# A gated line scan: its normaliser by Ln, Exp and one Newton step, its directions summed by identity matmuls

## The chip, the cores and the metric

One core of a Trainium2 chip runs the whole program in one launch. The metric is the device time in microseconds (us). Three runs of the kernel before took 17805.31, 17695.79 and 17706.48 us; their median is 17706.48 us.

## The reference

Two layers work on 8 images of 192 x 64 x 64, in float32. The change is in the first, a gated scan in four directions over 384 channels:

```
Gl, Gm, Gr = normalize_w(...)       # s = |Gl| + |Gm| + |Gr| + 1e-7; each of them / s
def step(h, inp):
    x, l, gl, gm, gr = inp          # one column of every chunk of 8
    h_up, h_dn = h shifted by one row down and up, zeros at the border
    hn = l * x + gl * h_up + gm * h + gr * h_dn
    return (hn, hn)
out = hs * Us + xs * Ds             # hs: all hidden states; xs: the input in 4 directions
y = einsum('bdchw,d->bchw', out by direction, w_m)
```

The gates, L, U and D are projections of a 16-channel proxy of the input. Behind the scan come two norms and a projection; the second layer is a window attention that keeps the 16 largest scores of a row, and an MLP.

## The kernel before

For each of the 8 images the program runs four stages. `front` projects the input and convolves it. `scan` works channel tile by channel tile (ct, 3 of 128 channels), step by step (t, 8), direction by direction (d, 4), each time on 512 tokens (64 rows x 8 chunks). `norms` takes the layer norm and the response norm. `window_row` (8 a image) does the second layer.

The scan of one direction at a step t > 0, with the lines of the kernel:

- TensorE projects three gates into one PSUM tile g of three banks (through the helper at L229), and L, D and U into tiles pl of one bank each. A projection has 16 rows: row groups at partitions 0, 32, 64 and 96 hold copies of the proxy.
- VectorE (DVE) multiplies L by the input (lx, L272). ScalarE (ACT) takes the absolute values of the gates (ab, L274). DVE multiplies the gates by the three shifted hidden states (pr, L276).
- GpSimd (POOL) adds two absolute values (L277), DVE adds the third and 1e-7 (L278) and takes the reciprocal (L281).
- POOL adds the three products (L282, L283) and multiplies by the reciprocal (L284). DVE adds lx, which is the new hidden state (`now`, L285).
- DVE multiplies D by the input (dx, L290) and U by the hidden state (hu, L294). POOL adds hu and dx to an accumulator in SBUF (L297, L299, L301); for the last direction the sum goes to y (L303).

At t = 0 there are no gates: L times the input is the hidden state (L269). The hidden states of the four directions are four tiles; the directions do not depend on each other, the steps do.

The program is written with symbolic tiles. A scheduler puts the instructions of each engine into one fixed order, and each engine works its queue in that order. A pool with one buffer makes the next tile wait until the last reader of the one before is done. PSUM has 8 banks, and the scan uses all: g has two buffers (6 banks), pl two.

Of the kernel before, what the change touches and what calls it, by code (L numbers as in the profile page):

```python
# [31 lines left out]
STRIP = 16  # image rows of one convolution strip  # L32
# [9 lines left out]
def tile_ss2d_then_window_attention(ctx: ExitStack, tc: tile.TileContext, a: dict, out: bass.AP):  # L42
    """Layer 0 (gated line scan in four directions) and layer 1 (top-16 window attention and MLP).

    Token orders of one image of 64 x 64, h = row, w = 8 c + t:
      scan order    (t, h, c): a step of the scan is 512 tokens in a row
      window order  (g, c, i, t), h = 8 g + i: a window is 64 tokens, a group 512, in a row
    Heads are taken as h = 2 r + j: r is the partition block of 32, j the block of 96 channels.
    """
# [17 lines left out]
    w_in = load("w_in")  # [96, 2, 384]  # L67
    w_dw = load("w_dw")  # [128, 3, 9]
    vecs = load("vecs")  # [128, 5, 3]: b_dw, gamma, beta, ln_w, ln_b
    w_xd = load("w_xd")  # [128, 3, 128]: x_proxy in four copies, 32 partitions apart  # L70
    w_g1 = load("w_g1")  # rows 0, 32, 64, 96: left, middle, right gate, L
    w_g2 = load("w_g2")  # rows 0, 32: D, U
    w_m = load("w_m", a["w_m"].partition_broadcast(48))
    w_out = load("w_out")  # [128, 3, 192]
    w_qk = load("w_qk")  # [96, 2, 384], columns (qk, j, r, d)
    b_qk = load("b_qk")  # [1, 384]
    w_v = load("w_v")  # [96, 2, 192], columns (j, r, d)
    b_v = load("b_v")  # [96, 2], rows (r, d), columns j
    w_pr = load("w_pr")  # [96, 2, 192], rows (r, d) of j
    b_pr = load("b_pr")  # [1, 192]  # L80
    n1_g = load("n1_g", a["n1_g"].partition_broadcast(P))
    n1_br = load("n1_br")  # [1, 192]
    n_cols = load("n_cols")  # [96, 3, 2]: norm1_b, norm2_g, norm2_b
    temp = load("temp", a["temp"].partition_broadcast(P))  # [128, 6], (j, r)
    rpb = load("rpb")  # [128, 3, 128], (window, query) x r x (j, key)
    w_f1 = load("w_f1")  # [96, 2, 768]
    b_f1 = load("b_f1")  # [128, 6]
    w_f2 = load("w_f2")  # [128, 6, 192]
    b_f2 = load("b_f2")  # [96, 2]
# [10 lines left out]
    nc.vector.memset(eps5, 1e-5)  # L100
    rpb_neg = const.tile([P, 3, P], F32, tag="rpb_neg", name="rpb_neg")
    nc.vector.tensor_scalar(rpb_neg, rpb, NEG, None, ALU.add)
    # One hidden state a direction, with a row of zeros above the image and one below it.
# [5 lines left out]
    with tc.tile_pool(name="prep", bufs=2) as prep, tc.tile_pool(name="prep_ps", bufs=2, space=PSUM) as prep_ps:  # L109
        # The direction's weight goes into its U and D.  # L110
# [3 lines left out]
        # W_out with its outputs' mean taken off, as the norm behind it does.  # L114
# [5 lines left out]
        # norm1's b is left out of the tokens: it goes into the biases of q, k, v and the shortcut.  # L120
# [4 lines left out]
        # v's bias comes out of the attention as it went in: it goes into the projection's.  # L125
# [16 lines left out]
        # norm2's g and b go into fc1.  # L142
# [78 lines left out]
    def scan(xa, xp, y):  # L221
        with (
            tc.tile_pool(name="scan", bufs=2) as pool,
            tc.tile_pool(name="gate_ps", bufs=2, space=PSUM) as gps,
            tc.tile_pool(name="lud_ps", bufs=2, space=PSUM) as lps,
# [11 lines left out]
            def directed(ct, d, t):  # L237
                """The scan's input of direction d at step t, [p, h, c] or [p, h / 8, h % 8, c]."""
                u = CH - 1 - t if d >= 2 else t
                if d % 2 == 0:  # L240
                    v = xa[:, ct, u * 512 : (u + 1) * 512].rearrange("p (i c) -> p i c", c=CH)
                else:
                    v = xa[:, ct, :].rearrange("p (il h ih) -> p ih il h", il=8, ih=8)[:, :, :, u::CH]
                if d >= 2:
                    v = v[:, :, ::-1] if d % 2 == 0 else v[:, :, :, ::-1]
                return v
# [6 lines left out]
            for ct in range(CT):  # L253
                y_ct = y[:, ct, :].rearrange("p (g c i t) -> p g i c t", g=NG, c=CH, i=WS)
                for t in range(CH):
                    acc = pool.tile([P, 512], F32, name="acc")
                    for d in range(ND):
# [3 lines left out]

                        if t > 0:
                            g = gps.tile([P, 3, 512], F32, name="g")
                            for r in range(3):
                                project(g[:, r, :], w_g1, r, ch, t)
                        pl = lps.tile([P, 512], F32, name="pl")
                        project(pl, w_g1, 3, ch, t)
                        if t == 0:
                            nc.vector.tensor_mul(as_directed(now, d), as_directed(pl, d), xv)  # L269
                        else:  # L270
                            lx = pool.tile([P, 512], F32, name="lx")
                            nc.vector.tensor_mul(as_directed(lx, d), as_directed(pl, d), xv)  # L272
                            ab = pool.tile([P, 3, 512], F32, name="ab")
                            nc.scalar.activation(ab, g, AF.Abs)  # L274
                            pr = pool.tile([P, 3, 512], F32, name="pr")
                            nc.vector.tensor_mul(pr, g, view(hid[d], [[CH, 3], [1, 512]]))  # L276
                            nc.gpsimd.tensor_add(ab[:, 0, :], ab[:, 0, :], ab[:, 1, :])  # L277
                            nc.vector.scalar_tensor_tensor(  # L278
                                ab[:, 0, :], ab[:, 2, :], 1e-7, ab[:, 0, :], ALU.add, ALU.add
                            )  # L280
                            nc.vector.reciprocal(ab[:, 0, :], ab[:, 0, :])  # L281
                            nc.gpsimd.tensor_add(pr[:, 0, :], pr[:, 0, :], pr[:, 1, :])  # L282
                            nc.gpsimd.tensor_add(pr[:, 0, :], pr[:, 0, :], pr[:, 2, :])  # L283
                            nc.gpsimd.tensor_mul(pr[:, 0, :], pr[:, 0, :], ab[:, 0, :])  # L284
                            nc.vector.tensor_add(now, pr[:, 0, :], lx)  # L285

                        pd = lps.tile([P, 512], F32, name="pl")
                        project(pd, w_g2, 0, ch, t)
                        dx = pool.tile([P, 512], F32, name="dx")
                        nc.vector.tensor_mul(as_directed(dx, d), as_directed(pd, d), xv)  # L290
                        pu = lps.tile([P, 512], F32, name="pl")
# [4 lines left out]
                        if d == 0:  # L296
                            nc.gpsimd.tensor_add(acc, hu, dx)  # L297
                            continue
                        nc.gpsimd.tensor_add(acc, acc, hu)  # L299
                        if d < ND - 1:  # L300
                            nc.gpsimd.tensor_add(acc, acc, dx)  # L301
                        else:
                            nc.gpsimd.tensor_add(  # L303
                                y_ct[:, :, :, :, t],
                                acc.rearrange("p (g i c) -> p g i c", g=NG, c=CH),
                                dx.rearrange("p (g i c) -> p g i c", g=NG, c=CH),
                            )

# [1 line left out]
    def norms(y, small, one):  # L310
        gx = small.tile([P, CT, NG], F32, name="gx")
        with tc.tile_pool(name="norms", bufs=2) as pool:
            for g in range(NG):
# [20 lines left out]
                # Tokens' scales from partitions to a row, the same on all partitions.  # L334
# [46 lines left out]
    def window_row(b, g, y, wz, bz, pool, small, one, three):  # L381
        def two_blocks(dst, src):
            """The transpose of [128 tokens, tile, 192] as [96 channels, 2, 512 tokens]."""
# [8 lines left out]
        # W_out and norm1  # L392
# [20 lines left out]
        # q and k, each head's to length one  # L413
# [21 lines left out]
        qkT = pool.tile([HALF, 4, GT], F32, name="qkT", bufs=1)  # blocks q0, q1, k0, k1  # L435
# [11 lines left out]
        # v, keys of a window on partitions, once for j = 0 and below for j = 1  # L447
# [16 lines left out]
        # scores: partitions (window of a pair, query), columns (r, pair, j, key); r has a bank  # L464
# [17 lines left out]
        # the 16th largest of each row  # L482
# [12 lines left out]
        # softmax of kept scores or -100, and the position bias  # L495
# [16 lines left out]
        # attention times v, as [(r, d), j, token]  # L512
# [25 lines left out]
        # projection, shortcut, norm2  # L538
# [28 lines left out]
        # MLP, by channels; x2 is added by transposing it onto fc2's sums  # L567
# [53 lines left out]
def _laid_out(i):  # L621
    """The inputs in the layouts that the program reads them in."""
# [16 lines left out]
    # Heads h = 2 r + j: channels (r, j, d) to (j, r, d).  # L639
# [55 lines left out]
```

## Time and profile before

| What | Value |
|---|---|
| median of three runs | 17706.48 us |
| span of the profiled execution, first to last instruction | 17788.9 us |
| the run of the three that is nearest above that span | 17805.31 us |
| busy over the whole span: PE, DVE, POOL, ACT | 12616.1, 8605.7, 5983.4, 3160.3 us |
| period of one image | about 2223 us |
| y of step 0 to y of the last step, in the scan of the first image (POOL L303) | 304.10 to 1137.79 us |
| the same, second image | 2542.66 to 3376.59 us |
| from y to y of a step: channel tile 0; tiles 1 and 2 | 39.95 us; 37.2 us |
| granted TensorE clock, mean over the span | 0.637 |

The profile is of one execution. PE is TensorE's matmuls, PEld its weight loads. A group line gives the busy time and mean duration of its instructions, then the engine's idle time just before them and who ended it. A float32 matmul shows as two MATMUL records, two passes. The clock is the share of full TensorE speed that the throttle granted; the profile shows 0.5 and 1.0, and means between. A timeline line gives start, duration (both us), engine, line, operation, tiles, shapes and count.

### The profile page before, as it was taken

The numbers are of one execution on the slowest core, as the hardware profiler recorded it, in microseconds if no ns is written. First come the engines' busy times: TensorE is split into PE (matmuls) and PEld (weight loads), VectorE is DVE, ScalarE is ACT, GpSimd is POOL, SyncE is SP. The second block draws the span as 40 slices with busy tenths as digits, with TensorE's granted clock in tenths as the row PEclk, the third lists the DMA queues.
The fourth block names the chain that finished last, engine by engine and source line by source line (L and its number), as shares of the span: only waits on it lengthen the run. The fifth ranks groups of instructions, "written<-read, shape, count | busy, mean of one in ns | idle before, by whom it ended". The sixth has DMA issues, their size and how long they took to land. (4 is left out here: it accounts for less than half of the span.)

```text
span 17788.9 us, 115154 instructions
## 1 busy us (share of the span) xinstructions
PE 12616.1 (71%) x44232; PEld 5933.9 (33%) x44232; DVE 8605.7 (48%) x14317; ACT 3160.3 (18%) x4337; POOL 5983.4 (34%) x4570
## 2 busy tenths in 40 slices
PE   8776687766876668776687766876668776687665
PEld 3233332333323333233332333323333233332333
DVE  3952239622395223962239522395223952249522
ACT  1112211122111221112211122111221112211122
POOL 2740027400274002740027400274002740027400
PEclk8556685566755668556685566755668556675566
DMA  0000000000000000000000000000000000000000
GB/s 18 0 0 4 3 9 0 0 4 3 9 0 0 4 3 9 0 0 4 3 9 0 0 4 3 9 0 0 4 3 9 0 0 4 4 8 0 0 4 4
DMA packets 23070, 64.52 MB, mean 4 GB/s; under 512 B 2707, under 2 KB 3286, under 8 KB 22518
## 3 DMA queue, kind: packets, MB, share of 16 engines
q1 hardware_dynamic: 21424, 54.68, 1.2%
q8 instruction: 347, 5.69, 0.1%
q10 hardware_dynamic: 1094, 2.48, 0.0%
q14 instruction: 205, 1.68, 0.0%
HBM read 31.98 MB, written 25.17 MB: 3 GB/s over the span
## 5 line engine op out<-in xcount | busy, mean ns | idle before, releaser
L229 PE MATMUL pl<-xp,w_g 16*128 16x512 f32 x4608 | 3811.1, 1124 | 1306.0 <-DVE dx L290 553.6
L229 PE MATMUL g<-xp,w_g 16*128 16x512 f32 x4032 | 2729.0, 1108 | 456.7 <-DVE pr L276 456.7
L281 DVE RECIPROCAL ab<-ab 128x512 f32<-128x512 f32 x672 | 2244.8, 3340 | 0.0
L501 POOL TENSOR_TENSOR at<-at,rpb 128x1536 f32<-128x1536 f32 x64 | 218.6, 3415 | 5967.1 <-DVE keep L491 5904.6
L229 PEld LDWEIGHTS pl<-xp,w_g 16*128 16x128 f32 x4608 | 1133.8, 307 | 3187.2 <-DVE dx L290 1322.6
L274 ACT ACTIVATE ab<-g 128x1536 f32<-128x1536 f32 x672 | 974.7, 1450 | 5678.3 <-POOL pr L284 5082.3
L518 PE MATMUL one<-ident,ex 128*128 128x128 f32 x768 | 197.2, 427 | 1980.9 <-POOL ex L510 1980.9
L229 PEld LDWEIGHTS g<-xp,w_g 16*128 16x128 f32 x4032 | 975.6, 315 | 1691.3 <-DVE pr L276 1146.5
L194 PE MATMUL pc<-xin,diag 128*128 128x512 f32 x3456 | 1499.3, 592 | 0.0
L276 DVE TENSOR_TENSOR pr<-g,hid 128x1536 f32<-128x1536 f32 x672 | 1175.0, 1749 | 6.5 <-ACT ab L274 6.2
L277 POOL TENSOR_TENSOR ab<-ab 128x512 f32<-128x512 f32 x672 | 850.0, 1265 | 941.3 <-ACT ab L274 941.3
L405 DVE RECIPROCAL ss<-ss 128x4 f32<-128x4 f32 x64 | 11.4, 178 | 2211.7 <-ACT ss L404 2211.7
L283 POOL TENSOR_TENSOR pr<-pr 128x512 f32<-128x512 f32 x672 | 990.4, 1474 | 52.7
L284 POOL TENSOR_TENSOR pr<-pr,ab 128x512 f32<-128x512 f32 x672 | 855.2, 1273 | 311.1 <-DVE ab L281 297.7
L189 DVE COPY xin<-pin 128x384 f32<-128x384 f32 x288 | 160.6, 558 | 1606.3 <-PE pin L182 1606.3
L194 PEld LDWEIGHTS pc<-xin,diag 128*128 128x128 f32 x3456 | 653.0, 189 | 810.1 <-issue 784.8
L282 POOL TENSOR_TENSOR pr<-pr 128x512 f32<-128x512 f32 x672 | 862.1, 1283 | 36.9 <-DVE pr L276 36.9
L578 PE MATMUL one<-hd,w_f 128*96 128x512 f32 x1536 | 809.4, 652 | 56.7 <-ACT hd L576 56.7
L572 PE MATMUL one<-xT,w_f 96*128 96x512 f32 x1536 | 848.0, 680 | 0.0
L518 PEld LDWEIGHTS one<-ident,ex 128*128 128x128 f32 x768 | 146.0, 219 | 2000.6 <-POOL ex L510 1989.6
L299 POOL TENSOR_TENSOR acc<-acc,hu 128x512 f32<-128x512 f32 x576 | 740.6, 1286 | 156.0 <-DVE hu L294 155.9
L285 DVE TENSOR_TENSOR hid<-pr,lx 128x512 f32<-128x512 f32 x672 | 510.3, 759 | 554.6 <-POOL pr L284 554.3
(154 smaller groups left out, 16751.0 us busy)
## 6 DMA issues: line engine op xcount, KB each, us to landing
out_dram<-ot SPq DMA_DIRECT2D x64, 384.0 KB, 3.0
xt<-in_x_dram SPq DMA_DIRECT2D x16, 864.0 KB, 7.4
xt<-in_x_dram SPq DMA_DIRECT2D x16, 816.0 KB, 5.8
w_f<-in_w_f_dram ACTq DMA_DIRECT2D x2, 576.0 KB, 7.5
w_g<-in_w_g_dram SPq DMA_DIRECT2D x1, 768.0 KB
w_g<-in_w_g_dram ACTq DMA_DIRECT2D x1, 768.0 KB
w_in<-in_w_in_dram SPq DMA_DIRECT2D x1, 288.0 KB, 3.3
w_out<-in_w_out_dram ACTq DMA_DIRECT2D x1, 288.0 KB, 10.3
```

Of the source, the lines that this page charges most:

```text
L194: nc.tensor.matmul(pc, lhsT=diag[:, ct, k, :], rhs=xin[:, 8 * hf + dy : 8 * hf + dy + 8, dx : dx + W], start=k == 0, stop=k == 8,)
L229: nc.tensor.matmul(dst, lhsT=w[32 * row : 32 * row + NS, ch : ch + P], rhs=xp[32 * row : 32 * row + NS, t, :], start=True, stop=True,)
L274: nc.scalar.activation(ab, g, AF.Abs)
L276: nc.vector.tensor_mul(pr, g, view(hid[d], [[CH, 3], [1, 512]]))
L277: nc.gpsimd.tensor_add(ab[:, 0, :], ab[:, 0, :], ab[:, 1, :])
L281: nc.vector.reciprocal(ab[:, 0, :], ab[:, 0, :])
L282: nc.gpsimd.tensor_add(pr[:, 0, :], pr[:, 0, :], pr[:, 1, :])
L283: nc.gpsimd.tensor_add(pr[:, 0, :], pr[:, 0, :], pr[:, 2, :])
L284: nc.gpsimd.tensor_mul(pr[:, 0, :], pr[:, 0, :], ab[:, 0, :])
L299: nc.gpsimd.tensor_add(acc, acc, hu)
L572: nc.tensor.matmul(ph, lhsT=w_f1[:, ci, m * P : (m + 1) * P], rhs=xT[:, ci, :], start=ci == 0, stop=ci == 1)
L578: nc.tensor.matmul(pf[k], lhsT=w_f2[:, m, k * HALF : (k + 1) * HALF], rhs=hd, start=m == 0, stop=False)
```

## The change

It touches `scan` (and adds a constant of 1e-7 per partition, eps7). The reciprocal r of s + 1e-7 becomes exp(-ln(s + 1e-7)) on ACT, followed by one Newton step. The sum s is put into the PSUM bank of the right gate; DVE works there. With rr the first estimate and p the sum of products, `gr` becomes (s + 1e-7) rr, then (gr - 2) (p rr), and the hidden state is lx - gr. The three gates lie in two tiles, g (two banks) and gr (one bank), so Abs and the product with the hidden state are two instructions each. L and D share a tile of two banks, U has a tile of its own, and the directions are summed in PSUM by matmuls with the identity: dx and hu of four directions make 8 matmuls onto one bank, and ACT copies it to y. Buffers: g 1 (2 banks), gr 2, L and D 1 (2 banks), U 1, acc 1; all 8 banks again.

```diff
-            tc.tile_pool(name="gate_ps", bufs=2, space=PSUM) as gps,
-            tc.tile_pool(name="lud_ps", bufs=2, space=PSUM) as lps,
+            tc.tile_pool(name="gate_ps", bufs=1, space=PSUM) as gps,
+            tc.tile_pool(name="right_ps", bufs=2, space=PSUM) as rps,
+            tc.tile_pool(name="ld_ps", bufs=1, space=PSUM) as lps,
+            tc.tile_pool(name="u_ps", bufs=1, space=PSUM) as ups,
+            tc.tile_pool(name="acc_ps", bufs=1, space=PSUM) as aps,
...
-                    acc = pool.tile([P, 512], F32, name="acc")
+                    acc = aps.tile([P, 512], F32, name="acc")
...
+                        ld = lps.tile([P, 2, 512], F32, name="ld")
+                        project(ld[:, 0, :], w_g1, 3, ch, t)
+                        project(ld[:, 1, :], w_g2, 0, ch, t)
+                        lx = now if t == 0 else pool.tile([P, 512], F32, name="lx")
+                        nc.vector.tensor_mul(as_directed(lx, d), as_directed(ld[:, 0, :], d), xv)
+                        dx = pool.tile([P, 512], F32, name="dx")
+                        nc.vector.tensor_mul(as_directed(dx, d), as_directed(ld[:, 1, :], d), xv)
...
-                            g = gps.tile([P, 3, 512], F32, name="g")
-                            for r in range(3):
-                                project(g[:, r, :], w_g1, r, ch, t)
...
+                            g = gps.tile([P, 2, 512], F32, name="g")
+                            gr = rps.tile([P, 512], F32, name="gr")
+                            project(g[:, 0, :], w_g1, 0, ch, t)
+                            project(g[:, 1, :], w_g1, 1, ch, t)
+                            project(gr, w_g1, 2, ch, t)
                             ab = pool.tile([P, 3, 512], F32, name="ab")
-                            nc.scalar.activation(ab, g, AF.Abs)
                             pr = pool.tile([P, 3, 512], F32, name="pr")
-                            nc.vector.tensor_mul(pr, g, view(hid[d], [[CH, 3], [1, 512]]))
+                            nc.scalar.activation(ab[:, 0:2, :], g, AF.Abs)
+                            nc.scalar.activation(ab[:, 2, :], gr, AF.Abs)
+                            nc.vector.tensor_mul(pr[:, 0:2, :], g, view(hid[d], [[CH, 2], [1, 512]]))
+                            nc.vector.tensor_mul(pr[:, 2, :], gr, view(hid[d], [[1, 512]], 2 * CH))
                             nc.gpsimd.tensor_add(ab[:, 0, :], ab[:, 0, :], ab[:, 1, :])
-                            nc.vector.scalar_tensor_tensor(
-                                ab[:, 0, :], ab[:, 2, :], 1e-7, ab[:, 0, :], ALU.add, ALU.add
-                            )
-                            nc.vector.reciprocal(ab[:, 0, :], ab[:, 0, :])
                             nc.gpsimd.tensor_add(pr[:, 0, :], pr[:, 0, :], pr[:, 1, :])
                             nc.gpsimd.tensor_add(pr[:, 0, :], pr[:, 0, :], pr[:, 2, :])
-                            nc.gpsimd.tensor_mul(pr[:, 0, :], pr[:, 0, :], ab[:, 0, :])
-                            nc.vector.tensor_add(now, pr[:, 0, :], lx)
...
+                            nc.vector.tensor_add(gr, ab[:, 0, :], ab[:, 2, :])
+                            rr = pool.tile([P, 512], F32, name="rr")
+                            nc.scalar.activation(rr, gr, AF.Ln, bias=eps7)
+                            nc.scalar.activation(rr, rr, AF.Exp, scale=-1.0)
+                            nc.vector.scalar_tensor_tensor(gr, gr, 1e-7, rr, ALU.add, ALU.mult)
+                            nc.gpsimd.tensor_mul(pr[:, 0, :], pr[:, 0, :], rr)
+                            nc.vector.scalar_tensor_tensor(
+                                gr, gr, 2.0, pr[:, 0, :], ALU.subtract, ALU.mult
+                            )
+                            nc.vector.tensor_sub(now, lx, gr)
...
+                        pu = ups.tile([P, 512], F32, name="pu")
                         project(pu, w_g2, 1, ch, t)
                         hu = pool.tile([P, 512], F32, name="hu")
                         nc.vector.tensor_mul(hu, pu, now)
...
-                        if d == 0:
-                            nc.gpsimd.tensor_add(acc, hu, dx)
-                            continue
-                        nc.gpsimd.tensor_add(acc, acc, hu)
...
+                        nc.tensor.matmul(acc, lhsT=ident, rhs=dx, start=d == 0, stop=False)
+                        nc.tensor.matmul(acc, lhsT=ident, rhs=hu, start=False, stop=d == ND - 1)
+                    nc.scalar.copy(y_ct[:, :, :, :, t], acc.rearrange("p (g i c) -> p g i c", g=NG, c=CH))
```

More of the change, by code (lines that the diff above doesn't have):

```diff
@@ L100, in tile_ss2d_then_window_attention @@
     nc.vector.memset(eps5, 1e-5)
+    eps7 = const.tile([P, 1], F32, tag="eps7", name="eps7")
+    nc.vector.memset(eps7, 1e-7)
     rpb_neg = const.tile([P, 3, P], F32, tag="rpb_neg", name="rpb_neg")
@@ L260, in scan @@
                         now = hid[d][:, CH : CH + 512]
-                        if t > 0:
-                            g = gps.tile([P, 3, 512], F32, name="g")
-                            for r in range(3):
-                                project(g[:, r, :], w_g1, r, ch, t)
[L266 to L272, printed above, removed]
+                        ld = lps.tile([P, 2, 512], F32, name="ld")
@@ L283, in scan @@
                             nc.gpsimd.tensor_add(pr[:, 0, :], pr[:, 0, :], pr[:, 2, :])
[L284 to L290, printed above, removed]
@@ L291, in scan @@
-                        pu = lps.tile([P, 512], F32, name="pl")
+                            nc.vector.tensor_add(gr, ab[:, 0, :], ab[:, 2, :])
[4 more added lines that the diff above has]
+                            nc.gpsimd.tensor_mul(pr[:, 0, :], pr[:, 0, :], rr)
@@ L294, in scan @@
                         nc.vector.tensor_mul(hu, pu, now)
-                        if d == 0:
-                            nc.gpsimd.tensor_add(acc, hu, dx)
-                            continue
-                        nc.gpsimd.tensor_add(acc, acc, hu)
[L300 to L307, printed above, removed]
+                        nc.tensor.matmul(acc, lhsT=ident, rhs=dx, start=d == 0, stop=False)
+                        nc.tensor.matmul(acc, lhsT=ident, rhs=hu, start=False, stop=d == ND - 1)
+                    nc.scalar.copy(y_ct[:, :, :, :, t], acc.rearrange("p (g i c) -> p g i c", g=NG, c=CH))
     def norms(y, small, one):
```

## The prediction

> **What bounds the kernel now.** I read the page's busy shares by slice first, then its groups, then the scan alone (the windows view), then single instructions (the timeline).
>
> ```profile
> DVE  3952239622395223962239522395223952249522
> PEclk8556685566755668556685566755668556675566
> ...
> L229 PE MATMUL pl<-xp,w_g 16*128 16x512 f32 x4608 | 3811.1, 1124 | 1306.0 <-DVE dx L290 553.6
> L229 PE MATMUL g<-xp,w_g 16*128 16x512 f32 x4032 | 2729.0, 1108 | 456.7 <-DVE pr L276 456.7
> L281 DVE RECIPROCAL ab<-ab 128x512 f32<-128x512 f32 x672 | 2244.8, 3340 | 0.0
> ```
>
> Eight images repeat. DVE is full (9) only in the scan, and there TensorE's granted clock is 5 tenths. A float32 matmul is two passes: the scan has 2304 `pl` and 2016 `g` matmuls, the page counts 4608 and 4032.
>
> ```profile
> 610.00:1150.00 540.00, 393.68 (x700) 148.42 (x697) 472.75 (x396) 77.00 (x54) 413.73 (x321) 0.50 0.00 0
> ```
>
> This is the scan's second and third channel tile: PE, PEld, DVE, ACT, POOL busy, then the clock. DVE is the bound (88%), PE is busy 73%, ACT 14%. One direction of one step t > 0 (a "turn" below; 84 an image, 672 in all) looks like this:
>
> ```profile
> 744.43 2.07 PE L229 MATMUL pl<-xp,w_g 16*128 16x512 f32 x2 [0.97 <-DVE dx L290]
> ...
> 746.11 0.69 DVE L285 TENSOR_TENSOR hid<-pr,lx 128x512 f32<-128x512 f32 x1 [1.74 <-POOL pr L284]
> 746.72 0.68 DVE L278 SCALAR_TENSOR_TENSOR ab<-ab 128x512 f32<-128x512 f32 x1
> 747.32 0.68 DVE L294 TENSOR_TENSOR hu<-pl,hid 128x512 f32<-128x512 f32 x1
> ...
> 747.92 0.68 DVE L272 TENSOR_TENSOR lx<-pl,xa 128x512 f32<-128x512 f32 x1
> ...
> 748.06 2.67 PE L229 MATMUL pl<-xp,w_g 16*128 16x512 f32 x4 [1.56 <-DVE hu L294]
> 748.52 3.34 DVE L281 RECIPROCAL ab<-ab 128x512 f32<-128x512 f32 x1
> ```
>
> A 512-wide DVE instruction takes 0.68 and the next starts 0.60 after it; one projection (x2) takes 2.07, two on different row groups (x4) 2.67, so the second costs 0.60. POOL's writes of y (L303) at 304.10 and 1137.79 enclose 833.7 us in every image: 84 turns and two t = 0 steps of some 13 each (a step and the t = 0 step behind it take 48.9 and 52.3 there against 37.2 for a step alone). A turn costs (833.7 - 27) / 84 = 9.6.
>
> **What goes, what comes.** Per turn DVE loses the reciprocal (3.26 from start to start) and L278, and splits L276 into 1024 and 512 elements (1.14 and 0.60); it gains the sum into PSUM and two Newton instructions. Its pitches add up to lx, dx 0.77 each (0.60, or 0.94 for the strided odd directions), 1.14, and six of 0.60: 6.3 against 8.3 before. POOL loses its acc adds (L297 to L303, 7 in four turns at 1.29) and keeps four instructions of 1.27 to 1.47: 5.3 against 7.6, hidden beside the rest then as now. ACT goes from one Abs (1.45) to 1.02 + 0.60, Ln 0.69 (as L576's 687 ns), Exp 0.62, a quarter of a strided y copy (1.14, as L202's 1139 ns) and two table loads of 1.28: 5.8, under any turn's length, so what counts of it is what others wait for. SP's queue and the DMAs do not change.
>
> In the built program ACT's order has a load ahead of every Ln and another ahead of every Exp, 1344 new ones. The trace has the price:
>
> ```profile
> 1499.46 0.58 ACT L390 COPY xT<-one 96x512 f32<-96x512 f32 x1 [0.27 <-PE one L387]
> 1500.06 1.28 ACT L576 ACT_TABLE_LOAD   x1
> ```
>
> It starts 0.02 after the copy ends and is over 1.28 later, before its Gelu's input is there. So Ln's load is hidden while ACT waits for the sum; Exp's is not, it stands between Ln and Exp: 1.28 on the path. The Trainium skill, "ScalarE: Activation LUTs" (What ACT_TABLE_LOAD costs), adds a drain of 1.38 to each load of 1.28, which speaks against this change; the two rows leave 0.02 for it. By that page 1.38 more would stand on the path, an estimate of 672 x 1.38 = 930 us if that path were the bound. The same page (Table sets) has one set with both functions, so that one load could do; the built order has two.
>
> **The path through DVE, ACT and POOL.** The built order works the directions nearly one after the other: sum, Ln, Exp, POOL product, second Newton, `now`, hu, the next direction's pr (1024), its sum. 0.69 + 1.28 + 0.62 + 1.27 + 0.69 + 0.69 + 0.60 + 1.14 + 0.69 = 7.7, and some 0.25 for four changes of engine (0.03 to 0.09 in the timeline): 7.9. lx, dx and the first Newton step fit under Ln, load, Exp and product. Two waits come on top. The sum reads SBUF twice, and DVE loses to POOL there:
>
> ```profile
> 315.67 1.26 POOL L282 TENSOR_TENSOR pr<-pr 128x512 f32<-128x512 f32 x1
> 315.79 1.69 DVE L278 SCALAR_TENSOR_TENSOR ab<-ab 128x512 f32<-128x512 f32 x1
> ```
>
> 0.68 becomes 1.69, ending 0.55 after POOL; where the order puts pr's third part between pr and sum (three turns in five) POOL's adds are running then: with their 1.27 each the sum ends 0.6, 1.3 and 1.9 later in those three, a mean of 0.8. And direction 0's Ln stands behind the y copy in ACT's queue, which waits for the last hu and its identity matmul: 2.07 + 1.14 + 1.28 = 4.5 after hu, where the sum is there after 2.4 to 3.7: about 1.5 once in four turns, a mean of 0.4. 7.9 + 0.8 + 0.4 = 9.1: against 9.6 that would be a small gain.
>
> **PE is late next.** Each turn gets two identity matmuls of 128 rows. Their price, from the norms:
>
> ```profile
> 1169.32 2.07 PE L342 MATMUL one<-dg,ones 128*128 128x512 f32 x2 [1.68 <-POOL dg L336]
> 1171.18 4.55 PE L317 MATMUL one<-y,mean 128*128 128x512 f32 x6
> ```
>
> 2.07 to the result, and the next starts 1.86 later. The 16-row projections above overlap; in these rows nothing runs beside a 128-row matmul, and I take it that nothing will. The built PE order of a turn is hu's identity, pu, dx's identity, then the gates, L and D: 3 x 1.86 = 5.6 in single file. The other five overlap by row groups: 1.86 + 4 x 0.60 = 4.3, together 9.9. In three turns of five the order cuts them in two (a gate of the next turn waits for DVE's pr ahead of hu's identity, its second half stands behind): 1.86 - 0.60 = 1.26 more, 11.1. Mean (3 x 11.1 + 2 x 9.9) / 5 = 10.6. g, ld, pu and acc have one buffer now, so PE cannot run ahead, and the y copy's 1.5 once in four turns stays bare, as pu and acc wait with it: 10.6 + 0.4 = 11.0. PE sets the pace; the 9.1 lie beside it.
>
> This holds while the clock stays at 0.50. Two windows with PE nearly always busy (span, PE busy, then clock):
>
> ```profile
> 1418.00:1437.00 19.00, 18.25 (x27) 0.50 0.00 1
> 1386.00:1402.00 16.00, 16.00 (x36) 0.99 0.00 0
> ```
>
> The first is q and k: 96-row matmuls (L419) with one-row ones (L422) between, 96% busy for 19 us, and the clock stays at half; the second is the MLP with 96 and 128 rows throughout, at full clock. The new scan mixes 128 rows and 16 rows, the former a third of the time (3.7 of 11.0): it is nearer to the first. I take 0.50. The Trainium skill, "TensorE: Matmul & The Clock Gate" (Part 1), says that about 3.4 us of sustained matmuls release the gate; 19 us did not do it in the first window. By that rule the scan would run at full clock and end as in rival 1, by an estimate.
>
> t = 0 steps: four directions in single file, each L, D, U (1.86 + 2 x 0.60) and two identities: 6.8, so 27 against 13, 14 more, three an image.
>
> Unknown is what DVE pays for writing PSUM: no row has it. Reading PSUM costs it nothing (hu 0.68, L285 0.69), so I take nothing; the other end is half speed for the in-place steps, 0.53 on the path each for sum and second Newton, 1.1 a turn, which makes the path 10.2, still under PE's 11.0. A gain is no more than the 0.08 of overlap per instruction.
>
> **Sum.** Per image 84 x (11.0 - 9.6) + 3 x 14 = 118 + 42 = 160; eight images 1280. Profiled span 17788.9 (a run near it took 17805.31, 16.4 around it), so about 19070 in that execution. Against the median 17706.48: 18990.
>
> **Rivals.**
> 1. Faster, the clock opens. If identities lift the scan's clock to 1.0, PE needs some 5.5 a turn and the path decides: 84 x (9.1 - 9.6) = -42 an image, -340: 17370. It decides once PE's turn falls under the path's 9.1, at a mean clock above 0.50 x 11.0 / 9.1 = 0.60. For it: PE's new density. Against: the q and k window.
> 2. PE packs better than I read it: no cut groups, 9.9 a turn and t = 0 overlapped with the last step of the tile before: 84 x 0.3 = 25 an image, 200: 17910; with half of the t = 0 cost 18080.
> 3. The waits add up instead of lying beside each other: path and PE in turn. Cut groups in every turn, the y copy, and PSUM writes at half speed: 11.1 + 0.4 + 0.8 = 12.3: 84 x 2.7 + 42 = 269, 2150: 19860.
> 4. The change does not take the reciprocal's place at all: excluded, the built order has no reciprocal in the scan.
>
> **How the numbers follow.** Forecast (18300 to 19500) 0.66; rival 1 0.12; rival 2 0.13, of which 0.06 within 1%; rival 3 0.09. The range 17950 to 19900 reaches from rival 2's middle to rival 3 and leaves out rival 1 and half of the first part of rival 2: under 2 in 10. A measurement here tells about 1% from no change. Faster 0.12, same 0.06, slower 0.82.
>
> **What would show it.** Right: in the scan PE's busy share in the nineties at a clock of 0.50, DVE's down to some 60%, waits of DVE on ACT (Ln, Exp) and of ACT's Abs on PE g; y to y some 44 a step instead of 37.2 to 39.95; 672 loads at the Exp line, 1.28 each; identities about 1.0 a pass. Wrong: a clock above 0.6 there, a step under 40, or PE idle on hu and the gates while the Ln-to-hu path has no gap.

## The result, and the profile after

The changed kernel takes 18943.88 us (median of 4 runs, 18917.27 to 18953.82) against 17705.44 of the kernel before on the same chip: ratio 1.068, 95% interval 1.065 to 1.072. It is slower by 1238 us, where 1280 more was forecast. Its profiled execution has a span of 18942.4 us (before 17788.9, an execution that lies 83 above its median, so that the two spans differ by 1153.5 only).

The page's busy totals, its two rows by slice, and its groups for the identities, the loads and the sum:

```profile
PE 14995.9 (79%) x47304; PEld 6121.3 (32%) x47304; DVE 7587.2 (40%) x15662; ACT 6043.7 (32%) x7889; POOL 4339.1 (23%) x3226
...
DVE  3652236522365223652236522365223652236522
...
PEclk8556675566755668556675566755667556675566
...
L309 PE MATMUL acc<-hu,ident 128*128 128x512 f32 x1536 | 1571.4, 1127 | 193.2 <-DVE hu L306 193.1
L308 PE MATMUL acc<-dx,ident 128*128 128x512 f32 x1536 | 1553.9, 1114 | 97.4 <-DVE dx L273 97.4
...
L291 DVE TENSOR_TENSOR gr<-ab 128x512 f32<-128x512 f32 x672 | 873.7, 1300 | 37.4
...
L294 ACT ACT_TABLE_LOAD x672 | 862.2, 1283 | 11.9
L295 ACT ACT_TABLE_LOAD x672 | 862.2, 1283 | 11.9
```

In the slice that lies wholly in the scan, the second of every five, DVE is no longer at 9 but at 6; the clock still shows 5 tenths there. In the windows view (length, then PE, PEld, DVE, ACT, POOL busy, clock) a stretch of the scan reads:

```profile
700.00:1100.00 400.00, 374.40 (x582) 103.79 (x582) 255.70 (x317) 194.64 (x213) 180.20 (x136) 0.51 0.00 0
```

PE is busy 94%, DVE 64%. TensorE's timeline shows how a turn is filled (start, duration):

```profile
857.68 2.07 PE L234 MATMUL g<-xp,w_g 16*128 16x512 f32 x2 [1.62 <-DVE pr L285]
859.68 2.08 PE L309 MATMUL acc<-hu,ident 128*128 128x512 f32 x2
861.69 2.07 PE L234 MATMUL pu<-xp,w_g 16*128 16x512 f32 x2
863.69 2.08 PE L308 MATMUL acc<-dx,ident 128*128 128x512 f32 x2
865.70 1.22 PE L234 MATMUL g<-xp,w_g 16*128 16x512 f32 x1
865.70 1.22 PE L234 MATMUL ld<-xp,w_g 16*128 16x512 f32 x2
865.72 1.22 PE L234 MATMUL gr<-xp,w_g 16*128 16x512 f32 x1
...
867.72 2.08 PE L309 MATMUL acc<-hu,ident 128*128 128x512 f32 x2
```

Every 2.0 us one thing begins: hu's identity, pu, dx's identity, then a group of four projections side by side. Nothing runs beside an identity, and the lone gate at 857.68 took a slot too. The copies of y (ACT L310) at 314.16 and 1291.84 enclose 977.7 us in the first image and 981.9 to 985.3 in the other seven, against 833.5 to 834.0 before: 149 more an image, 1193 in all. That is somewhat more than the 1153.5 between the two spans, so the loss lies in the scans; what lies between them became a little shorter.

In what follows a "turn" is again one direction of a step t > 0, as a quarter of the mean time from y to y, without the two intervals that end with the t = 0 step of a later channel tile and the two behind them; a t = 0 step is what such an interval and the one behind it take together, less a mean step, so it holds what the t = 0 step costs its neighbours too. Both are read from the first image. Busy shares are of the stretch 700 to 1100 us.

| Kernel | us | ratio, 95% interval | turn | t = 0 step | PE busy, clock |
|---|---|---|---|---|---|
| before | 17705 to 17783 by chip | 1 | 9.6 | 12 | 74%, 0.50 |
| changed | 18943.88 | 1.068, 1.065 to 1.072 | 11.0 | 26 | 94%, 0.51 |
| e1: no identities | 17457.71 | 0.986, 0.985 to 0.988 | 9.4 | 7 | 80%, 0.50 |
| e4: one identity a direction | 17698.86 | 0.999, 0.999 to 1.000 | 9.1 | 28 | 95%, 0.50 |
| e7: identities in bfloat16 | 17799.87 | 1.005, 1.004 to 1.007 | 9.6 | 19 | 89%, 0.50 |
| e5: 128-row projections | 17636.51 | 0.996, 0.994 to 0.997 | 9.3 | 18 | 83%, 0.95 |
| e6: 16-row identities | 18120.33 | 1.023, 1.022 to 1.025 | 9.9 | 22 | 80%, 0.50 |
| e11: the same, other rows | 18007.06 | 1.014, 1.012 to 1.016 | 9.7 | 16 | 69%, 0.50 |
| e3: no table loads | 18636.55 | 1.052, 1.051 to 1.054 | 10.5 | 29 | 96%, 0.50 |
| e2: reciprocal back | 19693.64 | 1.112, 1.110 to 1.114 | 12.2 | 22 | 94%, 0.51 |
| e9: only the normaliser, in SBUF | 18718.43 | 1.053, 1.051 to 1.055 | 11.1 | 9 | 63%, 0.50 |
| e8: e1 with more buffers | 17472.60 | 0.987, 0.985 to 0.988 | 9.4 | 5 | 77%, 0.50 |
| e10: e1 with two buffers of g | 17765.52 | 1.000, 0.999 to 1.001 | 9.8 | 7 | 74%, 0.50 |
| e12: e4, POOL sums at t = 0 | 17776.92 | 0.999, 0.998 to 1.000 | 9.4 | 18 | 95%, 0.50 |

### The profile page after: what moved, and what is told of

The parts are those of the page before. It is cut to its first block, busy times and chain, and to the rows that moved or that the text cites. A ratio compares the mean times of both kernels' runs of the same rounds, so it can differ in the third digit from the quotient of the medians.

```text
span 18942.4 us, 127028 instructions
## 1 busy us (share of the span) xinstructions
PE 14995.9 (79%) x47304; PEld 6121.3 (32%) x47304; DVE 7587.2 (40%) x15662; ACT 6043.7 (32%) x7889; POOL 4339.1 (23%) x3226
## 5 line engine op out<-in xcount | busy, mean ns | idle before, releaser
L234 PE MATMUL g<-xp,w_g 16*128 16x512 f32 x2688 | 2130.7, 1101 | 140.4 <-DVE pr L285 140.4
L234 PE MATMUL ld<-xp,w_g 16*128 16x512 f32 x3072 | 2092.2, 1092 | 115.3 <-DVE dx L273 109.9
L309 PE MATMUL acc<-hu,ident 128*128 128x512 f32 x1536 | 1571.4, 1127 | 193.2 <-DVE hu L306 193.1
L308 PE MATMUL acc<-dx,ident 128*128 128x512 f32 x1536 | 1553.9, 1114 | 97.4 <-DVE dx L273 97.4
L234 PE MATMUL pu<-xp,w_g 16*128 16x512 f32 x1536 | 1532.2, 1097 | 0.0
L283 ACT ACTIVATE ab<-g 128x1024 f32<-128x1024 f32 x672 | 687.5, 1023 | 2440.7 <-PE ld L234 692.4
L234 PE MATMUL gr<-xp,w_g 16*128 16x512 f32 x1344 | 1382.8, 1130 | 48.7 <-DVE hid L301 48.7
L297 POOL TENSOR_TENSOR pr<-pr,rr 128x512 f32<-128x512 f32 x672 | 849.3, 1264 | 1602.5 <-ACT rr L295 1602.5
L285 DVE TENSOR_TENSOR pr<-g,hid 128x1024 f32<-128x1024 f32 x672 | 820.5, 1221 | 528.7 <-ACT ab L283 528.3
L291 DVE TENSOR_TENSOR gr<-ab 128x512 f32<-128x512 f32 x672 | 873.7, 1300 | 37.4
L294 ACT ACT_TABLE_LOAD x672 | 862.2, 1283 | 11.9
L295 ACT ACT_TABLE_LOAD x672 | 862.2, 1283 | 11.9
```

The source lines that it names most:

```text
L234: nc.tensor.matmul(dst, lhsT=w[32 * row : 32 * row + NS, ch : ch + P], rhs=xp[32 * row : 32 * row + NS, t, :], start=True, stop=True,)
L285: nc.vector.tensor_mul(pr[:, 0:2, :], g, view(hid[d], [[CH, 2], [1, 512]]))
L291: nc.vector.tensor_add(gr, ab[:, 0, :], ab[:, 2, :])
L294: nc.scalar.activation(rr, gr, AF.Ln, bias=eps7)
L295: nc.scalar.activation(rr, rr, AF.Exp, scale=-1.0)
L297: nc.gpsimd.tensor_mul(pr[:, 0, :], pr[:, 0, :], rr)
```

## The experiments

The theory: the identities stand in TensorE's queue in single file at half clock, and TensorE sets the turn. Rival A (rival 2 in the expectations of e1 to e3): the table loads and the longer path through ACT set it. Rival B (rival 1 there): the buffers of which there is now only one do. Rival C, for later: something holds the clock at half that need not.

### Identities away, loads away, reciprocal back

**e1_pool_sum.** The changed kernel without identities: POOL sums as before, into acc in SBUF.

```diff
-                        nc.tensor.matmul(acc, lhsT=ident, rhs=dx, start=d == 0, stop=False)
-                        nc.tensor.matmul(acc, lhsT=ident, rhs=hu, start=False, stop=d == ND - 1)
+                        if d == 0:
+                            nc.gpsimd.tensor_add(acc, hu, dx)
+                            continue
+                        nc.gpsimd.tensor_add(acc, acc, hu)
...
```

> The normaliser by Ln, Exp and Newton stays, the directions are summed by POOL as before (acc in SBUF, one buffer), so no identity matmuls and no y copy on ACT. Theory (TensorE's throughput at half clock sets the pace): 4.0 us of TensorE time go from each turn of 11.0; the path through DVE, ACT and POOL is next, 7.9 + 0.8 = 8.7, and the t = 0 steps fall back to 13: 84 x (8.7 - 11.0) + 3 x (13 - 27) = -235 an image, 17060 us, up to 17500 if POOL's acc adds hold DVE's sum. Rival 1 (the single buffers of g, ld, pu make the waits): a turn stays above 10.3, 18400 or more. Rival 2 (table loads and Exp on the path): loads stay, so no gain but the y copy's 0.4, 18600 or more.

17457.71 us, at the upper end of what the theory gave, and faster than both kernels. The turn falls to 9.4 and a t = 0 step from 26 to 7. Two groups of its page, and the windows view:

```profile
L290 DVE TENSOR_TENSOR gr<-ab 128x512 f32<-128x512 f32 x672 | 962.5, 1432 | 1.4
L295 DVE SCALAR_TENSOR_TENSOR gr<-gr,rr 128x512 f32<-128x512 f32 x672 | 469.8, 699 | 1101.6 <-ACT rr L294 1101.6
```

```profile
700.00:1100.00 400.00, 320.70 (x516) 87.87 (x516) 308.54 (x388) 222.19 (x248) 321.27 (x246) 0.50 0.00 0
```

PE, DVE and POOL are at 80, 77 and 80%: no engine is full. DVE's sum, which reads SBUF twice, takes 1432 ns where it took 1300 with the identities, with POOL busy 80% instead of 45%. The new normaliser with its new split of PSUM is thus worth about 1.4% here, and the identities cost 8% on top. The split is not parted from the normaliser in this run; e9, below, has the normaliser without it.

**e2_recip.** The changed kernel with the reciprocal in SBUF in the place of Ln, Exp and Newton.

```diff
-                            nc.scalar.activation(rr, gr, AF.Ln, bias=eps7)
-                            nc.scalar.activation(rr, rr, AF.Exp, scale=-1.0)
...
+                            nc.vector.reciprocal(ab[:, 0, :], ab[:, 0, :])
```

> The identity matmuls and the buffers stay, the normaliser is DVE's reciprocal in SBUF again. Theory: TensorE's turn stays, 11.0, so within 1% of the changed kernel: 18750 to 19150. Rival 1: the same. Rival 2: without the loads, Ln and Exp the time falls back towards the kernel before, below 18200.

19693.64 us: rival A forecast a gain and is 1500 away, but the theory's is missed too, by 540. TensorE's timeline has the reason:

```profile
903.61 2.04 PE L234 MATMUL ld<-xp,w_g 16*128 16x512 f32 x2 [1.01 <-DVE dx L273]
905.58 2.08 PE L304 MATMUL acc<-hu,ident 128*128 128x512 f32 x2
907.59 2.07 PE L234 MATMUL pu<-xp,w_g 16*128 16x512 f32 x2
909.59 2.08 PE L303 MATMUL acc<-dx,ident 128*128 128x512 f32 x2
911.59 1.22 PE L234 MATMUL ld<-xp,w_g 16*128 16x512 f32 x1
...
913.46 1.91 PE L234 MATMUL g<-xp,w_g 16*128 16x512 f32 x2
915.74 2.04 PE L234 MATMUL ld<-xp,w_g 16*128 16x512 f32 x2 [0.37 <-DVE dx L273]
917.71 2.08 PE L304 MATMUL acc<-hu,ident 128*128 128x512 f32 x2
```

Six slots from 905.58 to 917.71, 12.1 us: the scheduler has put the work in another order, in which the other projections of the turn shown are cut into three groups. The expectation took the order as given; an edit on DVE had changed TensorE's.

**e3_no_loads.** Both functions become Identity, which needs no table.

```diff
-                            nc.scalar.activation(rr, gr, AF.Ln, bias=eps7)
-                            nc.scalar.activation(rr, rr, AF.Exp, scale=-1.0)
+                            nc.scalar.activation(rr, gr, AF.Identity, bias=eps7)
+                            nc.scalar.activation(rr, rr, AF.Identity, scale=1e-4)
```

> Ln and Exp are replaced by Identity activations of the same shapes (with Exp's scale 1e-4), which need no table load; so the hidden states are not the reference's, and all other instructions stand as in the changed kernel. Theory: only the direction behind the y copy gains, up to 0.4 a turn: 18650 to 18950. Rival 2: Exp's load of 1.28 goes from every turn, 672 x 1.28 = 860: 18080 or less. Rival 1: as the theory.

18636.55 us, 307 less than the changed kernel: 0.23 for each of the 1344 loads that went, of the 1.28 that each takes. Rival A fails here too; the theory's lower end is passed by 13 us. The loads are not free, but taking them away brings back only a quarter of the loss. In the first image the order of the instructions is that of the changed kernel; from the second on a few of them change places.

### How the price goes with the number and the kind of identity

**e4_one_ident.** POOL adds dx to hu, and one identity matmul takes the sum.

```diff
-                        nc.tensor.matmul(acc, lhsT=ident, rhs=dx, start=d == 0, stop=False)
-                        nc.tensor.matmul(acc, lhsT=ident, rhs=hu, start=False, stop=d == ND - 1)
+                        nc.gpsimd.tensor_add(hu, hu, dx)
+                        nc.tensor.matmul(acc, lhsT=ident, rhs=hu, start=d == 0, stop=d == ND - 1)
```

> POOL adds dx to hu, and one identity matmul a direction goes onto acc instead of two. Theory: 2.0 us of TensorE's time go from each turn of 11.0, which brings it to 9.0, level with the path of 9.1: a turn of 9.3 to 9.6, and 2 x 4 less in each t = 0 step: 84 x -1.55 - 3 x 8 = -154 an image, 17700 us (17400 to 18100). Rival 1: the chain of waits through acc, pu and hu is as long as before or longer by POOL's 1.27: 18800 or more. Rival 2: 18800 or more.

17698.86 us, as forecast. Two, one and no identity make 18944, 17699 and 17458: the first one taken away saves 1245 us, 1.85 a turn and so nearly one slot of 2.0; the second only 241. With no identity the turn even rises, from 9.1 to 9.4, with POOL, which adds everything, busy 80% instead of 68%; what falls is the t = 0 step, from 28 to 7. That step had been put 8 lower with one identity than with two, and it did not fall (26 and 28). The buffers of PSUM are those of the changed kernel, which speaks against rival B.

**e6_16_rows** and **e11_16_spread.** The identities take 16 rows, at 0 or at 64. The order of every engine is that of the changed kernel.

```diff
-                        nc.tensor.matmul(acc, lhsT=ident, rhs=dx, start=d == 0, stop=False)
-                        nc.tensor.matmul(acc, lhsT=ident, rhs=hu, start=False, stop=d == ND - 1)
+                        nc.tensor.matmul(acc, lhsT=ident[0:NS], rhs=dx[0:NS], start=d == 0, stop=False)
+                        nc.tensor.matmul(acc, lhsT=ident[0:NS], rhs=hu[0:NS], start=False, stop=d == ND - 1)
```

> The changed kernel with both identity matmuls over the first 16 rows only (the sum over directions covers 16 channels of each tile; this part is left out). Order, buffers, waits and the number of matmuls are as in the changed kernel. Theory (single file: a 128-row matmul leaves no room for another beside it): over 16 rows they overlap like the projections, the PE turn falls to 1.86 + 7 x 0.60 and two cuts, under 8, and the path sets the turn at about 9.2: (11.0 - 9.2) x 672 = 1210 less, and 24 t = 0 steps some 11 shorter, 260: about 17470 us, 17300 to 17750. Rival (the identities cost by what waits for them: single buffers of acc, ld, pu and dx held until they are done, and two more instructions in PE's queue): these all stay, so over 18600 us.

18120.33 us: nothing was taken from order, buffers, waits or count, only rows, and 824 us went. That is more than half of the 1486 that e1 gives back, so most of the cost is in the file, not in the waits. It is 370 more than the theory's upper end. In the timeline an identity now begins together with a projection:

```profile
917.76 1.06 PE L309 MATMUL acc<-hu,ident 16*128 16x512 f32 x1
917.76 1.22 PE L234 MATMUL pu<-xp,w_g 16*128 16x512 f32 x1
917.77 1.22 PE L234 MATMUL gr<-xp,w_g 16*128 16x512 f32 x1
```

At row 0 the two identities share a row group with a gate and with D. The next run moves them to the third gate's:

> The kernel with identities over 16 rows (18120 us, too slow for the theory) with these rows at 64 instead of 0 (the sum covers 16 other channels of each tile; the rest is left out). Order, buffers and waits unchanged. Theory: at row 0 both identities shared a row group with one gate and D, four matmuls in single file at half clock; at row 64 they share it with the third gate only, three at most and two in the other groups: the turn falls from 9.9 to 9.2 to 9.5, 17620 to 17900 us. Rival (the rest of the difference is the single buffers of acc, ld and pu): it stays at 18050 to 18200 us.

18007.06 us, between the two figures: 1.023 becomes 1.014. Sharing a row group explains part of what was missing. The rest (9.7 a turn against 9.3 in e5) is open; that matmuls at half clock also reach their readers a microsecond later (a lone pu takes 2.07 from start to end in the changed kernel, 1.02 in e5) would fit, but no run isolates it.

**e7_bf16_ident.** ident, dx and hu are bfloat16.

```diff
-                        dx = pool.tile([P, 512], F32, name="dx")
+                        dx = pool.tile([P, 512], BF16, name="dx")
...
-                        nc.tensor.matmul(acc, lhsT=ident, rhs=dx, start=d == 0, stop=False)
+                        nc.tensor.matmul(acc, lhsT=ident_h, rhs=dx, start=d == 0, stop=False)
...
```

> The changed kernel with ident, dx and hu in bfloat16, so that an identity matmul is one pass instead of two. The built order of PE changes with it: the gates are no longer cut in two in any turn. Theory (PE's slots set the turn): an identity takes one pass of about 1.0 in single file, the turn on PE is 1.0 + 2.0 + 1.0 + 1.86 + 4 x 0.60 = 8.3, under the path, which then sets about 9.2 a turn; t = 0 steps about 20 instead of 26: 672 x 1.8 + 24 x 6 = 1350 less, about 17600 us, 17400 to 17850. Rival (the identities cost by the waits on single buffers): over 18500 us.

17799.87 us, inside the theory's range: with as many identities, 1144 less. Part of it can be due to PE's other order, in which the gates are not cut. The expectation had their price wrong in the safe direction:

```profile
909.34 0.58 PE L312 MATMUL acc<-hu,ident_h 128*128 128x512 bf16 x1
...
909.85 2.07 PE L237 MATMUL pu<-xp,w_g 16*128 16x512 f32 x2
```

pu starts 0.51 after the identity, not 1.0: a bfloat16 identity takes a quarter of a float32 one.

### Why the clock stays at half

**e5_full_rows.** Every projection of the scan takes all 128 rows. All orders are those of the changed kernel.

```diff
-                    lhsT=w[32 * row : 32 * row + NS, ch : ch + P],
-                    rhs=xp[32 * row : 32 * row + NS, t, :],
+                    lhsT=w[:, ch : ch + P],
+                    rhs=xp[:, t, :],
```

> The changed kernel with every projection of the scan over all 128 rows (whole weight and whole xp, so that gates, L, D and U are sums over all row groups: this part of the arithmetic is changed). Every engine's order and every buffer are as in the changed kernel. It asks why the clock stays at 0.50 in the scan. Theory: the grant follows how much of the array is in use, and five of seven matmuls use 16 rows of 128. Then the clock goes to 0.95 or more in the scan, a slot takes about 1.0, eight of them 8.0 a turn, PE is no longer the bound and the path of some 9.2 sets the turn: 17400 to 17800 us. Rival: the gate stays shut for another reason (the short gaps, the order of two-pass matmuls). Then all eight are in single file at half clock, 8 x 2.0 = 16 a turn: 672 x 5.0 = 3400 more, and the t = 0 steps 20 slots of 2.0 instead of 26 us, 24 x 14 = 340: about 22700 us at a clock of 0.50.

17636.51 us, inside the theory's range and five thousand under the rival's. The page's clock row reaches 9 in the scan, and the windows view has 0.95:

```profile
PEclk9976699766997669976699766997669976699766
```

```profile
700.00:1100.00 400.00, 331.62 (x698) 133.50 (x697) 296.87 (x382) 234.04 (x258) 218.19 (x164) 0.95 0.00 0
```

Same instructions in the same order; only the rows changed, and the clock opened. The identities are all there, two a turn, and the turn is 9.3. So the half clock was a condition of the loss. With it gone PE is busy 83%, and the turn is near the 9.1 at which the prediction put the path; that the path sets it is likely, but no run shows it alone. A version that keeps the arithmetic, with zero-padded copies of the weights, was not tried.

### What the normaliser is worth, and what holds e1

**e9_norm_alone.** The kernel before, only its normaliser changed, in SBUF.

```diff
-                            nc.vector.reciprocal(ab[:, 0, :], ab[:, 0, :])
+                            rr = ab[:, 1, :]
+                            nc.scalar.activation(rr, ab[:, 0, :], AF.Ln, bias=eps7)
+                            nc.scalar.activation(rr, rr, AF.Exp, scale=-1.0)
+                            nc.vector.scalar_tensor_tensor(ab[:, 0, :], ab[:, 0, :], 1e-7, rr, ALU.add, ALU.mult)
...
```

> The kernel before with only the normaliser changed: sum, Ln, Exp and Newton step in SBUF (in ab), its buffers in PSUM and POOL's sums over directions as before. DVE's pitches fall from 8.3 to 6.3 a turn, POOL keeps 7.6. Theory (the reciprocal's place is worth most of the new path's gain, PSUM or not): 8.6 to 9.2 a turn, 0.4 to 1.0 less than before: 17050 to 17450 us. Rival (the sum and both Newton instructions now read SBUF twice and are each held up by POOL, 0.68 to as much as 1.69, so that keeping the normaliser in PSUM is what makes it pay): 3 x 0.7 = 2.1 more on DVE and on the path, 9.6 a turn or more: 17700 us or over.

18718.43 us: the rival, and by more than it gave. From its page:

```profile
L288 DVE SCALAR_TENSOR_TENSOR ab<-ab,pr 128x512 f32<-128x512 f32 x672 | 1141.2, 1698 | 305.1 <-POOL pr L287 305.1
L287 POOL TENSOR_TENSOR pr<-pr,ab 128x512 f32<-128x512 f32 x672 | 1133.3, 1687 | 162.7 <-ACT ab L283 161.4
L280 DVE TENSOR_TENSOR ab<-ab 128x512 f32<-128x512 f32 x672 | 1154.9, 1719 | 1.4 <-POOL ab L279 1.4
...
L282 ACT ACT_TABLE_LOAD x672 | 862.2, 1283 | 3435.2 <-DVE ab L280 3433.9
```

Sum and second Newton step read SBUF twice and take 1.7 each; in PSUM (e1) they take 1.43 and 0.69, and POOL's product 1.27. Beside it, ACT's one long Abs stands between Ln and Exp in the order. And Ln's load starts only when the sum is there (3435.2 us of waiting ahead of it), where in the changed kernel it ran before that (11.9), so both loads are now on the path. No engine is full (PE 63%, DVE 81%, POOL 72%): most of the turn of 11.1 is one ring of 10.5, load 1.28, Ln 0.72, Abs 1.43, load 1.28, Exp 0.63, product 1.71, Newton 1.74, sum 1.75. The runs do not part these costs, nor the place of the sum from the split of the gates into two tiles, which e1 has as well.

**e8_buffers** and **e10_gates_twice.** Two attempts to free e1.

```diff
-            tc.tile_pool(name="u_ps", bufs=1, space=PSUM) as ups,
+            tc.tile_pool(name="u_ps", bufs=2, space=PSUM) as ups,
...
-                        dx = pool.tile([P, 512], F32, name="dx")
+                        dx = pool.tile([P, 512], F32, name="dx", bufs=3)
...
-                            rr = pool.tile([P, 512], F32, name="rr")
+                            rr = ab[:, 1, :]
...
-                        hu = pool.tile([P, 512], F32, name="hu")
+                        hu = pool.tile([P, 512], F32, name="hu", bufs=3)
```

> The kernel without identity matmuls (POOL sums the directions, 17458 us) with more room: pu in two buffers (in the bank that acc left), dx and hu in three, rr in the second part of ab. It asks what holds that kernel at 9.3 a turn. Theory: POOL is busy 80% and DVE's lx and dx wait for POOL's sums to free dx; with a third buffer that wait goes and the path of about 8.5 to 9.0 sets the turn: 16900 to 17250 us. Rival: DVE and POOL slow each other whenever they meet, whatever the buffers: 17350 to 17500 us.

17472.60 us, as the rival had it; DVE's waits for POOL's sums were not what held the turn. Its timeline suggested a ring through the single g, which the next run cuts:

```diff
-            tc.tile_pool(name="gate_ps", bufs=1, space=PSUM) as gps,
+            tc.tile_pool(name="gate_ps", bufs=2, space=PSUM) as gps,
...
-            tc.tile_pool(name="ld_ps", bufs=1, space=PSUM) as lps,
-            tc.tile_pool(name="u_ps", bufs=1, space=PSUM) as ups,
+            tc.tile_pool(name="lud_ps", bufs=2, space=PSUM) as lps,
```

> The kernel without identity matmuls (POOL sums, 17458 us) with PSUM dealt out anew: the two gates of g in two buffers, and L, D, U in turn in two buffers as in the kernel before; the normaliser stays in PSUM. It asks what holds that kernel at 9.3 to 9.5 a turn. Theory: a ring through the one buffer of g: pr frees it, then 2.07 matmul, 1.02 Abs, 1.28 load, 0.69 Ln, 0.59 Abs, 1.28 load, 0.63 Exp, 0.70 first Newton, 1.22 pr, together 9.5. With two buffers of g the ring is cut and POOL's 8.0 is next: 8.2 to 8.8 a turn, 672 x 0.6 to 1.1 less: 16750 to 17100 us. Rival (DVE and POOL slow each other, the ring only follows from it): 17350 to 17500 us.

17765.52 us, by its ratio slower than e1 and outside both forecasts. The wait for g is gone, and the two banks that paid for it seem to be missed elsewhere. The groups of the stretch 700 to 1100:

```profile
L232 PE MATMUL pl<-xp,w_g 16*128 16x512 f32 x266 | 227.5, 1126 | 101.9 <-DVE lx L270 52.8 <-DVE dx L272 41.3 <-DVE hu L305 5.3
L232 PE MATMUL g<-xp,w_g 16*128 16x512 f32 x158 | 115.8, 1107 | 2.3 <-DVE pr L284 2.3
```

g waits 2.3 us in all, but L, D and U, three through two banks, wait 101.9. What sets e1's 9.4 is not settled.

**e12_hybrid.** e4 with the t = 0 steps summed by POOL.

```diff
+                        if t > 0:
+                            nc.gpsimd.tensor_add(hu, hu, dx)
+                            nc.tensor.matmul(acc, lhsT=ident, rhs=hu, start=d == 0, stop=d == ND - 1)
+                        elif d == 0:
+                            nc.gpsimd.tensor_add(acc, hu, dx)
+                        else:
...
```

> The kernel with one identity matmul a direction (POOL adds dx to hu, 17699 us) with the t = 0 steps summed by POOL in SBUF, without identity matmuls. With one identity a step t > 0 takes 36.0, less than the 37.4 of the kernel without any, but its t = 0 steps take some 28 (23.2 + 41.0 - 36.0) against 7.5 there. Theory (at t = 0 the identities stand in single file with L, D and U, so that this is all their cost, 24 times): 17699 - 24 x (28 - 10) = 17270 us, 17180 to 17400, under both kernels and under the one without identities (17458). Rival (the time of the t = 0 steps is the fill and drain of the single buffers, and moves to their neighbours): 17550 to 17750 us.

17776.92 us, no difference from before, and a miss for the theory. By its ratio, 0.999, it is level with e4, near what the rival gave, by which the time moves to the neighbours. The t = 0 steps fell from 28 to 18, a little over half of what was hoped. But an ordinary step takes 40.1 in the first channel tile, 37.8 in the second and 36.0 in the third, where e4 had 36.0 in all three: the same instructions, in three orders that the scheduler chose. The best kernel remains e1, 17458.

## Why the prediction was right

The likeliest case came: slower, PE late next, in the single file and at the clock named. The bound, the file and the clock were right; that the turn was hit to a tenth is luck, as errors offset each other. Point by point:

- **PE sets the turn.** Right. 11.0 a turn forecast, 11.0 measured. Identities, PE busy 94% and DVE 64% are as announced; taking rows (e6), passes (e7) or instructions (e4, e1) from the identities each gave time back.
- **The turn's composition.** Terms were off both ways. A slot is 2.0, not 1.86, and a group of four projections costs one slot, where five were put at 4.3: the turn from 859.68 to 867.72 takes 8.0, where 9.9 was forecast. A cut costs more than 1.26: a slot of 2.0 and often a wait, such as the 1.62 for pr ahead of the gate at 857.68. Five turns from 859.68 to 914.25 take 54.6, between 8.0 and 15.2 each.
- **The clock stays at 0.50.** Right, and for the reason given: the mix of rows, not gaps. e5 shows it. The Trainium skill, "TensorE: Matmul & The Clock Gate" (Part 1), lets some 3.4 us of sustained matmuls release the gate; the changed scan with PE busy 94% did not release it, the same order with 128 rows did. In this case the rows in use decide.
- **The path lies beside it at 9.1.** It fits: with the clock open and both identities in place the turn is 9.3.
- **The t = 0 steps.** 27 forecast, 26 measured, but the working is not borne out: by it half of the identities would make it some 8 shorter, and e4 has 28; with identities of 16 rows it is still 22 (e6), without any 7 (e1). The sum of single slots met the number by chance. What makes these steps long is open. The first y comes 10 later (304.10 to 314.16) where 14 was given.
- **The sum held up by POOL.** 0.8 forecast; 1.30 instead of 0.69, so 0.6.
- **The loads.** 672 at each line, 1.28 each, starting 0.02 after the operation before; Exp starts 0.01 after its load ends:

```profile
903.02 0.69 ACT L294 ACTIVATE rr<-gr,eps 128x512 f32<-128x512 f32 x1 [0.29 <-DVE gr L291]
...
903.73 1.28 ACT L295 ACT_TABLE_LOAD   x1
...
905.02 0.63 ACT L295 ACTIVATE rr<-rr 128x512 f32<-128x512 f32 x1
905.68 0.70 DVE L296 SCALAR_TENSOR_TENSOR gr<-gr,rr 128x512 f32<-128x512 f32 x1 [1.50 <-ACT rr L295]
```

  The drain of 1.38 that the page on "ScalarE: Activation LUTs" adds is not there. Beside PE most of a load is hidden (e3: 0.23 of 1.28). That Ln's load lies ahead of the sum is a matter of the order: in e1 and e9 it starts behind it.
- **DVE writing PSUM taken as free.** Right: 0.70 in place (last line above), against 0.68 in SBUF. The prediction did not see a gain in it: with one input in PSUM the instruction stays at 0.70 beside POOL, where e9's second Newton step, with both in SBUF, takes 1.70.
- **Rivals.** The open clock was priced at 17370; e5 opened it by other means and took 17637. Better packing came in part, four projections in one slot, and the cut turns took it back: waits did add up there, and the mean stayed at 11.0.

## What to carry to other kernels

Work moved to an engine with idle time is priced by the slot that it takes there, not by the engine's busy share: TensorE was 26% idle, but what it ran lay side by side in row groups, and two full-row matmuls a turn broke the file up. Look at the granted clock of the very stage before giving TensorE float32 work, and ask whether bfloat16 will do for it. And when a change is two changes, try them apart: here the kernel without the identities won 1.4%, and they lost it six times over.

## What the runs showed of the hardware

- The clock followed the rows in use: 0.51 with 16-row projections and two 128-row identities a turn, PE busy 94%; 0.95 with 128 rows throughout, same order.
- At clock 0.50 a 512-column matmul of 128 rows took a slot of 2.0 us in float32 and 0.51 in bfloat16.
- In e9 DVE instructions with both inputs in SBUF took 1.70 to 1.75 beside POOL instead of 0.68, and POOL's own 1.27 became 1.69; in e1 and the changed kernel, with one input in PSUM, DVE stayed at 0.70.
- A table load took its 1.28 and no more, even twice in every turn; whether it ran before its input was there or behind it differed from order to order.
